# A selective-scan kernel: a step of the scan in two halves, each with its own decays, and other work cut at half steps

## The chip, the cores and the metric

The kernel runs on one core of a Trainium2 chip. The metric is the device time of one launch in microseconds (us). Inside the core, five engines work side by side, each with its own queue of instructions: TensorE (PE in the profile; its weight loads are PEld), VectorE (DVE), ScalarE (ACT), GpSimd (POOL) and SyncE (SP), which here only issues DMAs. They meet through semaphores.

## The reference, cut to what matters

The input x is 8 images of 384 channels and 32 x 32 pixels, in fp32. Four layers follow one another, each as `x = x + layer(group_norm(x))`:

```python
# layers 0 and 2: a Mamba block over the 1024 pixels of an image, 768 inner channels, 16 states each
xin, z = split(xseq @ in_proj_w.T)
u  = silu(causal_conv3(xin) + conv_b)
dt, Bm, Cm = split(u @ x_proj_w.T);  dt = softplus(dt @ dt_proj_w.T + dt_proj_b)
def step(h, inp):
    dA = jnp.exp(dt_t[..., None] * A)                      # the decay of each state
    h = dA * h + (dt_t * u_t)[..., None] * B_t[:, None, :]
    y = jnp.einsum('bdn,bn->bd', h, C_t)
    return (h, y)
y = (scan(step) + u * D) * silu(z);   out = y @ out_proj_w.T
# layer 2 has a layer norm ahead of this and an MLP (384 -> 1536 -> 384, gelu) behind it
# layer 1: 1x1 conv, filter in the frequencies of 8x8 patches, 3x3 depthwise conv, gated, 1x1 conv
# layer 3: 3x3 depthwise conv
```

## The kernel before

**Chunks and steps.** An image is scanned in two chunks of 512 pixels, c = 0 and c = 1; the second starts from the states that the first leaves in `carry`. With 8 images and two Mamba layers there are 32 chunks, numbered n: 0 to 15 belong to layer 0, 16 to 31 to layer 2. A chunk has 768 x 16 states; 128 partitions hold 8 channels x 16 states, and a step scans four such groups, j = 0 to 3, so a chunk has 24 steps and the kernel 768. Three steps in four continue the same block k of 128 channels (`QUADS`).

**One step**, in the loop at the end (L1007 to L1039), t being the step:
- `times` (L619), GpSimd: `g`, which a DMA (`begin`, L610) has filled with dt*u copied over the states, is multiplied by B, in two instructions.
- `decay` (L627), TensorE and ScalarE: four matmuls, each on its own 32 rows of the array, copy dt over the states into the four PSUM banks `dA0` to `dA3`; then four Exp make the decays in place. There is one set of these banks, so the matmul for j of step t+1 must wait until VectorE has done with `dA[j]` of step t.
- `scan` (L637), VectorE: four scans. Those of j = 0 and 1 (`SHARE`) are written over `dA[j]` and VectorE multiplies them by C (L654); those of j = 2 and 3 are written over `g`, and GpSimd multiplies both by C in one instruction (L660) once the last is there. Where c = 0 the last column goes to `carry` (L653, L656).
- `gather` (L664), TensorE: four matmuls sum over the states into `y`; after the fourth step of a block one more adds u*D, and VectorE multiplies y by the gate (L676).

**All else** (norms, projections, gates, output projection, layer 1, MLP, layer 3) is written as generators in a list, `Jobs` (L90). A generator yields after a piece of work. `mm` and the `Meter` count what a piece takes of TensorE and VectorE, in us of a full-speed engine. In each step `jobs.begin` sets the room, `ROOM` (5.2 us of TensorE and 3.0 of VectorE in layer 0, 6.4 and 3.0 in layer 2), and pieces are taken in the order of the jobs' ends (`last`, in steps) while they fit. `NEXT` keeps a job back until the next step, `EARLY` marks a piece that is run right after the scan (a Silu or Gelu, with table loads), `WAIT` says that it can't go on. `jobs.until` runs pieces in order of their ends, past any room, until something that the scan needs is there.

**What sets the order.** [...] TensorE's part of step t is: jobs (up to 2.0 us), `gather` of t-1, the DMA of t+3 (`begin`, on SP), more jobs, and then the four decays of t+1. VectorE's is: the four scans and two multiplications of t, the vector part of the jobs, the gate. A piece of a job usually holds both a matmul group and the VectorE instruction that reads its result (`both`, L222), so the two are issued next to each other.

**Names used below.** `front` prepares a chunk (load, group norm, `layer_norm`, `ps_in`, Silu, `ps_x`, `ps_dt`), `gates` makes z, `finish` holds the output projection and, in layer 2, the MLP; `measure` takes the statistics of the next image through two buffers `spm`, which `layer_norm` and the `ps_dt` part of `front` use too; `live["spm"]` keeps them apart. `NBANK` (3) PSUM banks, `ps`, serve all jobs.

Of the kernel before, what the change touches and what calls it, by code (L numbers as in the profile page):

```python
# [16 lines left out]
P = 128  # L17
# [9 lines left out]
T = 512  # L27
# [21 lines left out]

SHARE = {"l0_": ((2, 2, 2, 2), (2, 2, 2, 2)), "l2_": ((2, 2, 2, 2), (2, 2, 2, 2))}  # L50
# [13 lines left out]
WAIT = "wait"  # L64
NEXT = "next"
EARLY = "early"

ROOM = {"l0_": (5.2, 3.0), "turn": (6.4, 3.0), "l2_": (6.4, 3.0)}
# [21 lines left out]
class Jobs:  # L90
# [3 lines left out]

    def __init__(self, work):
        self.work, self.jobs, self.needs = work, [], {}
        self.room = [0.0, 0.0]

    def add(self, kind, gen, first, last):
        self.jobs.append({"kind": kind, "gen": gen, "first": first, "last": last, "had": [], "got": None})  # L100
# [5 lines left out]
    def piece(self, job):  # L106

        before = list(self.work)
        got = next(job["gen"], self)
        if got is WAIT:  # L110
            return False
        took = tuple(x - y for x, y in zip(self.work, before))
        job["had"].append(took)
        self.room = [x - y for x, y in zip(self.room, took)]
        job["got"] = got
        if got is self:
            self.needs[job["kind"]] = job["had"]
            self.jobs.remove(job)
        return True
# [4 lines left out]
    def begin(self, room):  # L124
        self.room = [max(min(x, y / 8), -y) + y for x, y in zip(self.room, room)]
        early = [job for job in self.in_order() if job["got"] is EARLY]
        for job in self.jobs:
            if job["got"] is NEXT:
                job["got"] = None
        if early:  # L130
            self.piece(early[0])

    def step(self, t, most=None):

        most = most and self.work[0] + most
        went = True
        while went and not (most and self.work[0] >= most):
            went = False
            for job in self.in_order():
                need = self.need(job)  # L140
                if job["got"] is None and job["first"] <= t and all(
                    y == 0 or x >= y - 0.1 for x, y in zip(self.room, need)
                ):
                    went = self.piece(job)
                    if went:
                        break

    def until(self, done):

        while not done():  # L150
            if not any(self.piece(job) for job in self.in_order()):
# [4 lines left out]
def tile_conv_preact_d4(ctx: ExitStack, tc: tile.TileContext, a: dict, out: bass.AP):  # L156
# [10 lines left out]
    live = {"ps": 0, "dt": 0, "x": 0, "spm": False}  # L167
# [21 lines left out]
    def pipe(units, deep=2):  # L189
# [3 lines left out]
        units = deque(units)  # L193
        while units or flying:
            went = bool(flying)
            for f in list(flying):
                if f["stages"]:
                    f["stages"].popleft()(f["ps"])
                settle(f)
                if not f["stages"]:  # L200
                    flying.remove(f)
            if units and live["ps"] < NBANK and len(flying) < deep:
# [4 lines left out]
                stages[0](ps)  # L207
                f = {"stages": deque(stages[1:]), "ps": ps, "bank": True}
                settle(f)
                if f["stages"]:  # L210
                    flying.append(f)
            if units or flying:
                yield None if went else WAIT

    def settle(f):
        if f["bank"] and (not f["stages"] or f["stages"][0] is None):
            f["bank"] = False
            ps_done()
            if f["stages"]:
                f["stages"].popleft()  # L220
# [59 lines left out]
    def group_stats(block, all_read=lambda: None, between=None):  # L280
# [13 lines left out]
        yield NEXT  # L294
# [69 lines left out]
    def depthwise(pool, rows, todo):  # L364
# [12 lines left out]
        yield NEXT  # L377
        for q, (n, t) in enumerate(taps):
            if t == 0:
                ps = yield from ps_tile("ps_dw")  # L380
            _, window, take = todo[n]
# [5 lines left out]
            if t == 8:  # L387
                take(ps[:rows])
# [10 lines left out]
    def measure(s):  # L399
# [12 lines left out]
        live["spm"] = True  # L412
# [7 lines left out]
        def all_read():  # L420
            live["spm"] = False

        s["stats"] = yield from group_stats(block, all_read, NEXT)
# [36 lines left out]
    def layer_norm(xn):  # L460
        ps = yield from ps_tile("ps_ln")
        for k in range(KC):
            mm(ps, ln_mean, xn[:, k, :], start=k == 0, stop=k == KC - 1)
        for k in range(KC):
            vector.tensor_sub(xn[:, k, :], xn[:, k, :], ps)
        ps_done()
        yield NEXT
        while live["spm"]:
            yield WAIT
        ps = yield from ps_tile("ps_lv")  # L470
        for k in range(KC):
            sq = wk.tile([P, T], F32, tag="spm", name="sq", bufs=2)
            act(sq, xn[:, k, :], AF.Square)
            mm(ps, ln_mean, sq, start=k == 0, stop=k == KC - 1)
        rsqrt(ps, ps, eps_ln)
        yield
# [5 lines left out]
        yield NEXT  # L482
        for k in range(KC):
            act(xn[:, k, :], xn[:, k, :], AF.Identity, bias=ln_b[:, k : k + 1])
        yield NEXT

    def front(s):

        c, n = s["c"], s["n"]
        while n > 0 and ("gates", 1) not in chunks[n - 1]:  # L490
            yield WAIT
# [8 lines left out]
        yield NEXT  # L500
# [18 lines left out]
        def taps(d):  # L519
# [10 lines left out]
            ("ps_in", [both(project(s, d, 0), tap(d), taps(d))]) for d in range(ND)  # L530
        )
        if c > 0:
# [16 lines left out]
        yield NEXT  # L549
        ps = yield from ps_tile("ps_x")  # L550
        for d in range(ND):
            mm(ps[:RX, :], w["x"][:, d, :], u[d], start=d == 0, stop=d == ND - 1)
        dbc = wk.tile([RX, T], F32, tag="dbc", name="dbc")
        act(dbc, ps[:RX, :], AF.Identity, bias=one_row)
        ps_done()
        yield NEXT
# [9 lines left out]
        def step_dt(d):  # L566
# [10 lines left out]
            def plus(ps):  # L577
                v = s["dt"][d] = wk.tile([P, T], F32, tag="dt", name="dt", bufs=NDT)
                vector.scalar_tensor_tensor(v, ps, 0.0, got["m"], ALU.max, ALU.add)

# [11 lines left out]
            return [both(log, plus), None, both(times_u, spill)]  # L592
# [3 lines left out]
        flying = []  # L596
        for d in range(ND):
            while live["dt"] >= NDT or live["spm"]:
                yield WAIT
            live["dt"] += 1  # L600

            flying.append(pipe([("ps_dt", step_dt(d))]))
            flying = [f for f in flying if next(f, f) is not f]
            yield NEXT
        while flying:
            flying = [f for f in flying if next(f, f) is not f]
            yield NEXT
# [19 lines left out]
    def decay(s, i):  # L627
        k, sub = QUADS[i]
        for j in range(4):
            rows = slice(32 * j, 32 * (j + 1))  # L630
            mm(dAs[j], selr[rows, sub, :], s["dt"][k][rows, :])
        if sub == NSUB - 1:
            live["dt"] -= 1
        for j in range(4):
            act(dAs[j], dAs[j], AF.Exp, scale=s["w"]["A"][:, 4 * i + j : 4 * i + j + 1])

    def scan(s, i):  # L637

        g = s["g", i]
        own = SHARE[s["pre"]][s["c"]][i % NSUB]  # L640
        for j in range(4):
            q = 4 * i + j
            nc.vector.tensor_tensor_scan(  # L643
                dAs[j] if j < own else g[:, j, :],
# [6 lines left out]
            if j < own:  # L651
# [3 lines left out]
        if s["c"] < NCH - 1:  # L655
            nc.vector.tensor_copy(  # L656
                carry[:, 4 * i + own : 4 * i + 4].unsqueeze(2), g[:, own:4, T - 1 : T]
            )
        g = g[:, own:4, :]
        nc.gpsimd.tensor_mul(  # L660
            g, g, s["bc"][:, 1, :].unsqueeze(1).to_broadcast([P, 4 - own, T])
        )

    def gather(s, i):  # L664
# [8 lines left out]
        if sub == NSUB - 1:  # L673
            u = s["u"][k // NH][:, k % NH, :]
            mm(y, s["w"]["D"][:, k, :], u, start=False)
            nc.vector.tensor_mul(u, y, s["z", k // NH][:, k % NH, :])  # L676
# [4 lines left out]
    def out_proj(s):  # L681
# [24 lines left out]
        def stages(m):  # L706
            if last:
# [3 lines left out]
                both(part(m, 1), lambda ps: vector.tensor_add(x[:, m, :], ps, x[:, m, :])),  # L711
            ]

        yield from pipe(("ps_out", stages(m)) for m in range(KC))
        s["free"] = True

    def finish(s):

        yield from out_proj(s)
# [6 lines left out]
        if s["pre"] == "l2_":  # L726
            if s["c"] == NCH - 1:
                jobs.add("layer3", layer3(s), 0, t + 3 * NQ - 1)
        elif s["c"] == NCH - 1:
            until = 2 * NQ + 3 if s["n"] == B * NCH - 1 else 3 * NQ - 2  # L730
# [34 lines left out]
    def patch_pair(xl, hb, pp):  # L765
# [28 lines left out]
        return pixels, both(frequencies, filtered), back  # L794

    def layer1(s):
# [3 lines left out]
        for hb in range(H // PS):  # L800
# [11 lines left out]
            yield NEXT  # L812
            for stages in zip(*(patch_pair(xl, hb, pp) for pp in range(2))):
                yield from pipe(("ps_t", [stage]) for stage in stages)
                yield NEXT
        for hf in range(2):
            gate = p1.tile([Q96, 2, 512], F32, tag="acc", name="gate")

            def some(j):
# [9 lines left out]
                return w1dw[:, j, :], window, take  # L829
# [6 lines left out]
            yield NEXT  # L836

            def outward(m):
# [8 lines left out]
                return [both(run, lambda ps: vector.tensor_add(xc, ps, xc))]  # L847

            yield from pipe(("ps_o1", outward(m)) for m in range(KC))
            yield  # L850
# [40 lines left out]
    def mlp(s):  # L891
# [12 lines left out]
        for half in range(2):  # L904
# [30 lines left out]
            yield NEXT  # L935

            def down(m):
# [20 lines left out]
                return [sum_up(0, 0), sum_up(0, 1), sum_up(1, 0), both(sum_up(1, 1), add)]  # L958

            yield from pipe([("ps_dn", down(m)) for m in range(KC)], deep=1)  # L960

    def layer3(s):
# [3 lines left out]
        for k in range(KC):  # L966
# [4 lines left out]
            for hf in range(2):  # L971
# [10 lines left out]
                yield from depthwise(p2, P, [(dw3[:, k, :], window, take)])  # L982
# [23 lines left out]
    decay(*steps[0])  # L1006
    for t in range(total):  # L1007
# [3 lines left out]
        if i == 0:  # L1011
            jobs.add("gates", gates(s, 1), t + 1, t + 8)
            if s["c"] == 0 and n + NCH < len(chunks):
                jobs.add("measure", measure(chunks[n + NCH]), t, t + NQ + 4)
            if later:
                jobs.add("front%d" % (later["pre"] == "l2_"), front(later), t + 3, t + 14)
                jobs.add("gates", gates(later, 0), t + 13, t + NQ + 2)
        if i == 3 and n == B * NCH:
            load_diagonal(s["w"], s["pre"])
        if i % (NH * NSUB) == NSUB:  # L1020
            jobs.until(lambda: ("gates", i // (NH * NSUB)) in s)
        if t + 1 < total:
            times(*steps[t + 1])
        scan(s, i)
        jobs.begin(ROOM["turn" if n == B * NCH else s["pre"]])
        jobs.step(t, 2.0)
        if t > 0:
            p, q = steps[t - 1]
            gather(p, q)
            if q == NQ - 1:  # L1030
                end = 10 if p["pre"] == "l0_" else 23 if p["c"] == 0 else 16
                jobs.add("end%d" % (p["pre"] == "l2_"), finish(p), t + 1, t + end)
        if t + AHEAD < total:
            p, q = steps[t + AHEAD]
            jobs.until(lambda: p.get("dud", {}).get(QUADS[q][0]))
            begin(p, q)
        jobs.step(t)
        if t + 1 < total:
            decay(*steps[t + 1])  # L1039
    gather(*steps[-1])  # L1040
    jobs.add("end1", finish(steps[-1][0]), 0, total)
# [131 lines left out]
```

## Time and profile before

| | |
|---|---|
| median of 3 runs | 7926.02 us (7921.78 to 7940.09) |
| the profiled execution | 7942.61 us, its span 7940.8 us |
| before the first scan / after the last scan | 92.4 us / 192.5 us |
| 14 chunks of layer 0 (n = 2 to 15, 336 steps) | 490.0 to 3574.4 us: 9.18 us a step |
| turn from layer 0 to 2 (n = 16 to 21) | 3574.4 to 5230.4 us |
| 9 chunks of layer 2 (n = 22 to 30, 216 steps) | 5230.4 to 7523.7 us: 10.62 us a step |
| busy in the span: PE, DVE, ACT, POOL | 7334.3, 5717.7, 4052.0, 5639.5 us |

The stretches are read off the timeline: a chunk begins with the first of its 96 scans. A busy engine is one that has an instruction in flight[...].

### The profile page before, as it was taken

The page shows a single profiled execution, that of the slowest core. Times are in us where ns is not written, and L with a number is a line of the kernel's source. Part 1 is how long each engine was busy: PE and PEld are TensorE (multiplying, and loading weights), DVE is VectorE, ACT ScalarE, POOL GpSimd, SP SyncE. Part 2 cuts the span into 40 slices and gives each one's busy share as a digit, 9 for nine tenths or more (in the row PEclk, how much of TensorE's full clock was granted, in tenths as well). Part 3 has the DMA queues.
Part 4 walks back from the last instruction along what each step waited for, and adds up shares of the span by engine and source line. Part 5 has one row for each costly group of instructions (what it writes and reads, how often), then busy time and mean ns, then how long its engine had stood idle before and what let it go on. Part 6 is the DMA issues. An engine that isn't in the chain of part 4 may idle for free. (4 is left out here: it accounts for less than half of the span.)

```text
span 7940.8 us, 76871 instructions
## 1 busy us (share of the span) xinstructions
PE 7334.3 (92%) x25954; PEld 3037.2 (38%) x25954; DVE 5717.7 (72%) x7254; ACT 4052.0 (51%) x6980; POOL 5639.5 (71%) x2710
## 2 busy tenths in 40 slices
PE   7989999999998999989999989999899989999898
PEld 2223333333333333333334444444444444344445
DVE  5988788878787878778737647767767676676770
ACT  4445545555555555554544545555555555555553
POOL 5888888877787878777737746767767667676770
PEclk8888888989898999989889989999999999999999
DMA  5665655555564656556526645666656666565662
GB/s 138 148 148 137 144 135 136 134 133 137 133 149 118 146 129 143 122 141 151 122 69 173 159 121 144 154 158 165 157 134 163 166 149 159 138 171 140 168 157 65
DMA packets 289704, 1122.90 MB, mean 141 GB/s; under 512 B 37402, under 2 KB 91754, under 8 KB 191004
## 3 DMA queue, kind: packets, MB, share of 16 engines
q1 hardware_dynamic: 289308, 1117.98, 57.2%
q8 instruction: 205, 3.36, 0.2%
q14 instruction: 191, 1.56, 0.1%
HBM read 1042.34 MB, written 75.50 MB: 141 GB/s over the span
## 5 line engine op out<-in xcount | busy, mean ns | idle before, releaser
L623 POOL TENSOR_TENSOR g<-g,bc 128x1024 f32<-128x1024 f32 x1536 | 3586.5, 2357 | 181.3 <-DMA g<-dud 164.4
L660 POOL TENSOR_TENSOR g<-g,bc 128x1024 f32<-128x1024 f32 x768 | 1805.8, 2351 | 1609.5 <-DVE carry L656 871.8
L241 ACT ACTIVATE dA<-dA,w_A 128x512 f32<-128x512 f32 x3072 | 1858.3, 661 | 1480.3 <-PE dA L177 1467.3
L177 PE MATMUL dA<-dt,selr 32*128 32x512 f32 x6144 | 1521.9, 676 | 67.8 <-DVE g L654 59.2
L643 DVE TENSOR_TENSOR_SCAN dA<-dA,carry,g 128x512 f32<-128x512 f32 x768 | 986.7, 1285 | 750.5 <-issue 375.4
L643 DVE TENSOR_TENSOR_SCAN dA<-dA,g 128x512 f32<-128x512 f32 x768 | 940.8, 1225 | 554.3 <-ACT dA L241 221.6
L654 DVE TENSOR_TENSOR g<-dA,bc 128x512 f32<-128x512 f32 x1536 | 1054.5, 687 | 29.8 <-DVE dA L643 0.5
L177 PE MATMUL y<-g,sely 128*32 128x512 f32 x6144 | 934.2, 640 | 47.6 <-POOL g L660 42.4
L643 DVE TENSOR_TENSOR_SCAN g<-dA,carry,g 128x512 f32<-128x512 f32 x768 | 940.4, 1266 | 0.0
L643 DVE TENSOR_TENSOR_SCAN g<-dA,g 128x512 f32<-128x512 f32 x768 | 893.7, 1206 | 0.0
L177 PEld LDWEIGHTS dA<-dt,selr 32*128 32x128 f32 x6144 | 452.1, 192 | 947.2 <-DVE g L643 473.9
L177 PE MATMUL ps_up<-t,mw 128*128 128x256 f32 x2304 | 605.4, 411 | 144.4 <-ACT h L241 100.5
L177 PE MATMUL ps_dn<-h,mw 128*128 128x256 f32 x2304 | 566.1, 397 | 67.7 <-DMA mw<-in_l_mlp_w 55.9
L177 PE MATMUL ps_z<-xf,w_in 128*128 128x512 f32 x1152 | 590.0, 653 | 27.8 <-DVE dt L85 24.0
L177 PE MATMUL ps_dw<-tp,diag 96*96 96x512 f32 x1152 | 580.7, 645 | 14.3 <-ACT diag L241 14.3
L177 PEld LDWEIGHTS ps_up<-t,mw 128*128 128x128 f32 x2304 | 444.9, 201 | 371.0 <-ACT h L241 186.7
L177 PE MATMUL ps_in<-xf,w_in 128*128 128x512 f32 x1152 | 556.2, 623 | 25.3 <-DVE u L85 22.0
L177 PE MATMUL ps_out<-u,w_out 128*128 128x512 f32 x1152 | 548.7, 623 | 9.1 <-DVE x L85 9.1
L177 PEld LDWEIGHTS ps_dn<-h,mw 128*128 128x128 f32 x2304 | 436.7, 196 | 260.3 <-issue 121.0
L177 PE MATMUL ps_dw<-xp,diag 128*128 128x512 f32 x864 | 405.4, 620 | 41.0 <-ACT diag L241 40.9
L241 ACT ACTIVATE h<-ps_up,vec 128x256 f32<-128x256 f32 x384 | 177.3, 474 | 442.7 <-PE ps_up L177 442.4
L241 ACT ACTIVATE u<-ps_in,w_vec 128x512 f32<-128x512 f32 x192 | 149.4, 778 | 478.1 <-PE ps_in L177 478.1
(98 smaller groups left out, 6514.5 us busy)
## 6 DMA issues: line engine op xcount, KB each, us to landing
g<-dud SPq DMA_DIRECT2D x768, 1024.0 KB, 7.1
mw<-in_l_mlp_w SPq DMA_DIRECT2D x384, 384.0 KB, 7.2
dud<-du SPq DMA_DIRECT2D x768, 64.0 KB, 1.7
xk<-in_x SPq DMA_DIRECT2D x48, 256.0 KB, 4.1
xf<-in_x SPq DMA_DIRECT2D x16, 768.0 KB, 8.5
x<-in_x SPq DMA_DIRECT2D x16, 768.0 KB, 8.4
x_mid<-x SPq DMA_DIRECT2D x16, 768.0 KB, 4.7
xk<-x_mid SPq DMA_DIRECT2D x48, 256.0 KB, 5.4
```

Source lines behind the costliest of these rows:

```text
L177: nc.tensor.matmul(out_, lhsT, rhs, start=start, stop=stop)
L241: nc.scalar.activation(out_, in_, func, **kw)
L623: nc.gpsimd.tensor_mul(g, g, s["bc"][:, 0, :].unsqueeze(1).to_broadcast([P, 2, T]))
L643: nc.vector.tensor_tensor_scan(dAs[j] if j < own else g[:, j, :], dAs[j], g[:, j, :], 0.0 if s["c"] == 0 else carry[:, q : q + 1], ALU.mul ...
L654: nc.vector.tensor_mul(g[:, j, :], dAs[j], s["bc"][:, 1, :])
L660: nc.gpsimd.tensor_mul(g, g, s["bc"][:, 1, :].unsqueeze(1).to_broadcast([P, 4 - own, T]))
```

## The change

**The step.** `decay` and `scan` take a tuple of j. A step is now: `times` of t+1; scans 0 and 1 of t; decays 0 and 1 of t+1; `gather` of t-1; `begin` of t+3; half a step of jobs; scans 2 and 3 of t; decays 2 and 3 of t+1; the gate of t-1 (`gated`, taken out of `gather`); the other half of the jobs. Scans with odd j are written over `dA[j]` and multiplied by VectorE, those with even j go to `g`; GpSimd's multiplication comes after scan 2, ahead of scan 3. `SHARE` goes.

**The jobs.** `Jobs.begin` and `Jobs.step` become `half`, with a room for each half: 2.2 and 3.2 us of TensorE in layer 0 (5.4 a step), 3.0 and 3.9 in layer 2 (6.9); VectorE 1.0 each. A piece is taken if half of what it needs is there, and what it takes too much is owed. A new mark, `HALF`, keeps a job back until the next half step; it replaces most `NEXT`, and stands between a matmul group and the VectorE instruction that reads it, in `pipe`, `front`, `layer_norm`, `depthwise`, `out_proj`, layer 1 and the MLP. `EARLY` pieces run at the beginning of a second half.

**The list.** `out_proj` becomes a job of its own, with its end 6 steps after the chunk; `finish` (MLP) is added when it is done. Other ends: `gates` 4 steps (before 8), `front` 11 (14), layer 1 and layer 3 8 to 11 steps earlier. `until` takes the job that is waited for first. `live["spm"]` counts, so that two `ps_dt` units are under way at a time, and in `layer_norm` the squares are made ahead of the matmuls that read them.

```diff
-    def begin(self, room):
-        self.room = [max(min(x, y / 8), -y) + y for x, y in zip(self.room, room)]
...
+    def half(self, t, room, early):
+
+        self.now += 1
+        self.room = [min(x, 1.5) + y for x, y in zip(self.room, room)]
+        for job in self.in_order():
+            if early and job["early"] and job["at"] <= self.now:
+                self.piece(job)
+                break
...
+                    and all(y == 0 or x >= y / 2 for x, y in zip(self.room, self.need(job)))
...
-    def until(self, done):
+    def until(self, done, kind=None):
         while not done():
-            if not any(self.piece(job) for job in self.in_order()):
+            late = [job for job in self.in_order() if job["kind"] == kind]
+            if not any(self.piece(job) for job in late + self.in_order()):
...
-    def decay(s, i):
+    def decay(s, i, js):
         k, sub = QUADS[i]
-        for j in range(4):
+        for j in js:
             rows = slice(32 * j, 32 * (j + 1))
             mm(dAs[j], selr[rows, sub, :], s["dt"][k][rows, :])
...
-    def scan(s, i):
+    def scan(s, i, js):
...
-                dAs[j] if j < own else g[:, j, :],
+                dAs[j] if j % 2 else g[:, j, :],
...
+            elif j:
+                if s["c"] < NCH - 1:
+                    nc.vector.tensor_copy(
+                        carry[:, 4 * i : 4 * i + 4 : 2].unsqueeze(2), g[:, 0:4:2, T - 1 : T]
+                    )
+                nc.gpsimd.tensor_mul(
+                    g[:, 0:4:2, :], g[:, 0:4:2, :],
+                    s["bc"][:, 1, :].unsqueeze(1).to_broadcast([P, 2, T]),
+                )
...
-        scan(s, i)
-        jobs.begin(ROOM["turn" if n == B * NCH else s["pre"]])
-        jobs.step(t, 2.0)
-        if t > 0:
-            p, q = steps[t - 1]
-            gather(p, q)
...
-        jobs.step(t)
-        if t + 1 < total:
-            decay(*steps[t + 1])
+        scan(s, i, (0, 1))
+        if t + 1 < total:
+            decay(*steps[t + 1], (0, 1))
+        if t > 0:
+            gather(*steps[t - 1])
+        if t + AHEAD < total:
+            p, q = steps[t + AHEAD]
+            jobs.until(
+                lambda: p.get("dud", {}).get(QUADS[q][0]), "front%d" % (p["pre"] == "l2_")
+            )
+            begin(p, q)
+        jobs.half(t, room[0], False)
+        scan(s, i, (2, 3))
+        if t + 1 < total:
+            decay(*steps[t + 1], (2, 3))
...
+            gated(p, q)
             if q == NQ - 1:
-                end = 10 if p["pre"] == "l0_" else 23 if p["c"] == 0 else 16
-                jobs.add("end%d" % (p["pre"] == "l2_"), finish(p), t + 1, t + end)
...
+                jobs.add("out%d" % (p["pre"] == "l2_"), out_proj(p), t + 1, t + 6)
+        jobs.half(t, room[1], True)
```

## The prediction

> **What bounds the kernel now.** I read first the page's busy times, its slices and the busy times by stretch.
>
> ```profile
> PE 7334.3 (92%) x25954; PEld 3037.2 (38%) x25954; DVE 5717.7 (72%) x7254; ACT 4052.0 (51%) x6980; POOL 5639.5 (71%) x2710
> ...
> PE   7989999999998999989999989999899989999898
> ...
> PEclk8888888989898999989889989999999999999999
> ```
>
> ```profile
> core 0: us, PE busy (x) PEld busy (x) DVE busy (x) ACT busy (x) POOL busy (x), PEclk, DMA share, GB/s
> ...
> 490.00:3574.40 3084.40, 2924.42 (x9739) 1032.04 (x9736) 2483.98 (x3148) 1628.03 (x2930) 2464.30 (x1184) 0.90 0.57 136
> ...
> 5230.40:7523.70 2293.30, 2106.55 (x8197) 990.84 (x8196) 1601.66 (x2081) 1214.05 (x2005) 1584.57 (x759) 0.96 0.61 154
> ```
>
> TensorE is the busiest engine everywhere. A layer-0 step (336 in the first stretch) takes 9.18 us: VectorE is busy 7.39 of it, GpSimd 7.33. A layer-2 step (216) takes 10.62: 7.42 and 7.34. So no other engine sets the pace on average, and in layer 0 TensorE's clock is 0.90. The next view is TensorE's decays alone (same columns, PE first), and three pieces of its timeline.
>
> ```profile
> 490.00:3574.40 3084.40, 762.70 (x2687) 227.24 (x2688) 2075.26 (x2353) 816.96 (x1345) 0.90 0.57 136
> 5230.40:7523.70 2293.30, 313.68 (x1728) 91.47 (x1728) 1333.71 (x1537) 517.90 (x865) 0.96 0.61 154
> ```
>
> ```profile
> 3006.21 2.00 PE L177 MATMUL dA<-dt,selr 32*128 32x512 f32 x8
> ```
>
> ```profile
> 5762.99 1.14 PE L177 MATMUL dA<-dt,selr 32*128 32x512 f32 x8
> 5764.06 2.84 PE L177 MATMUL ps_dw<-xp,diag 128*128 128x512 f32 x6
> ```
>
> Decays keep TensorE busy 762.7/336 = 2.27 us a step in layer 0, 313.7/216 = 1.45 in layer 2. With all four banks free they need 1.07 us until the next matmul starts (5762.99 to 5764.06). The rest, 1.20 us a step in layer 0, is waiting for VectorE that the busy time hides. The waits say the same, and show the other direction:
>
> ```profile
> ACT dA L241 <- PE dA L177: 1467.3, 852, 16.8
> ...
> DVE dA L643 <- issue: 553.5, 258, 11.4
> PEld dA L177 <- DVE g L643: 473.9, 668, 1.7
> ...
> DVE dA L643 <- ACT dA L241: 346.9, 123, 9.1
> ...
> DVE acc L85 <- PE ps_dw L177: 233.8, 35, 20.8
> ```
>
> TensorE waits for the last scan and then VectorE for TensorE and Exp. VectorE also waits for job results ("acc <- ps_dw") with scans queued behind. In the worst place a forced `front` holds all scans for 20 us:
>
> ```profile
> 3303.91 4.41 DVE L85 SCALAR_TENSOR_TENSOR u<-ps_in,w_vec,u 128x511 f32<-128x511 f32 x6
> ...
> 3328.61 0.69 DVE L85 SCALAR_TENSOR_TENSOR dt<-ps_dt,spm 128x512 f32<-128x512 f32 x1 [13.56 <-ACT spm L241]
> ...
> 3331.03 1.23 DVE L643 TENSOR_TENSOR_SCAN dA<-dA,g 128x512 f32<-128x512 f32 x1
> ```
>
> [...]
>
> **The change part by part.** The sum is made on the profiled execution (7942.6 us; 7940.8 of it span); it lies 16.6 us above the median, which is taken off at the end.
>
> *Decays in pairs: a cost.* Two pairs in place of one four, each with two rounds: 2 x 1.07 = 2.14 us. Bounds for the pair: 0.54, half of the four, if time went with the count; 1.07, if rounds set it. I take 1.07[...].
> - Layer 0: TensorE without decays 2924.4 - 762.7 = 2161.7; with 336 x 2.14 = 719 it is 2881, against 3084: room for 203 us.
> - Layer 2: 2106.6 - 313.7 = 1792.9; with 216 x 2.14 = 462 it is 2255, against 2293: room for 38 us only. Here 1.45 us become 2.14, on the bounding engine.
>
> *The turnaround goes off the path: the gain.* Exp of scans 0 and 1 of t+1 runs while VectorE is at scans 2 and 3 of t. A half of VectorE is 1.28 + 1.28 + 0.69 + a carry = about 3.4 us; pair and two Exp take 1.07 + 2 x 0.66 = 2.4, so about 1 us is spare. But TensorE now meets VectorE twice a step. Half A holds for it 1.07 + gather 1.00 + jobs 2.2 (3.0) = 4.3 (5.1) us, half B 1.07 + 3.2 (3.9) = 4.3 (5.0); both are over 3.4, and balanced. Pieces are lumps of up to 2.6 us (three matmuls, six records of 0.43), so some meetings miss. The mean wait at a meeting, w, isn't in this trace: 0, if the lumps are absorbed by the 1 us spare; 0.6, half of today's 1.20, if each meeting inherits its share. I take 0.12, near the lower end, because the forced pieces and the waits for job results go too (below). That is 0.24 x 336 = 81 us in layer 0 and 52 in layer 2.
>
> *Vector work a half step later.* Removed are stalls of the kind "acc <- ps_dw" (233.8), "dt <- spm" (143.9), "x <- ps_dn" (140.8); no instruction is added. A `ps` bank is held half a step longer; with three of them the price, if TensorE runs out of banks, is one late piece. Both go into w.
>
> *Gather, begin, gate, multiplication by C.* Gather moves ahead of the first jobs and behind two decays; what it reads was made a half step earlier. `begin` with its 1 MB DMA (7.1 us) goes out earlier on SP, nearly a step more than it needs. GpSimd starts L660 one scan and a multiplication (2.0 us) earlier, its 7.3 us a step then stand against 8.5; the price if it is late is its 164 us of waiting for `g`, today small. Gate and the L656 copy only change place. x and the MLP's weights are still loaded where `out_proj` starts, which in layer 2 is earlier in the chunk; their 8.4 and 7.2 us lie beside its 15 us of matmuls. All at 0.
>
> *Ends, until, squares ahead.* `until` took 33.4 us at the place shown, of which TensorE idled some 10, and VectorE's debt then made light steps; gone, but that is in the room counted above. `ps_lv` took 76.7 + 40.2 idle = 117 us for 16 uses, 7.3 each, against 6 x 0.43 = 2.6; I credit 3 us a use, 27 in the nine layer-2 chunks. The turn takes 1656 us for six chunks, 126 more than six of layer 2 (3 x 510); an earlier layer 1 takes perhaps half of that: 60.
>
> *Clock.* [...] Bounds: no change, or 0.95 and 0.98. I take 0.93 in layer 0 (2161.7 x 0.03/0.93 = 70) and 0.97 in layer 2 (19).
>
> *Sum.* Layer 0: 203 - 81 + 70 = 192 for 14 chunks, 219 for 16. Layer 2: 38 - 52 + 27 + 19 = 32 for nine, 36 for ten. Turn 60. Together 315: 7942.6 - 315 - 16.6 = 7611, said as 7610. Prologue and tail (92.4 and 192.5) stay.
>
> **The rivals.**
> - *Much faster.* w near 0 and clocks 0.95 and 0.98: layer 0 203 + 114 = 317, 362 for 16; layer 2 38 + 27 + 37 = 102, 113 for ten; turn 60: 7390. For it: VectorE and GpSimd leave 1.8 us a step free. Against: their sum per step is steady, the lumps of TensorE are not.
> - *Slower: two meetings a step.* Without the clock's help the gain is 203 x 16/14 + 65 x 10/9 + 60 = 364 us, and each us of w costs 672 x 16/14 + 432 x 10/9 = 1248. So it decides at w = 0.29 us. For it: TensorE can't run ahead past a decay, so a late VectorE job or a 5.5 us Silu piece on ScalarE (two table loads of 1.28, two Silu of 1.48) holds it twice; layer 2 has hardly any room. At w = 0.45 with the turn unchanged: 364 - 60 - 562 = -258, 8180. Against: the balance of the halves.
> - *No difference*: layer 0's gain paid back in layer 2, w near 0.29: 7926.
> - *The pair is cheaper than 1.07* (a decay doesn't do what I say): at 0.54 the 768 steps need 1.07 less each, and with TensorE the bound about half of that shows: 7200; it stands at the far end of much faster.
>
> **How the numbers follow.** Forecast 0.50 (its own range 7430 to 7800), much faster 0.18, no difference 0.07, slower 0.25. Below 7330 I leave about 0.07, above 8120 about 0.12. What a measurement can tell from no change is about 0.2%, 16 us. Faster by more: 0.50 + 0.18 + 0.02 of no difference = 0.70; same 0.03; slower 0.25 + 0.02 = 0.27.
>
> **What would show it.** TensorE's decays near 2.14 us a step in both layers, with a pair at 1.07 to the next matmul; layer-0 steps near 8.6 us, layer-2 steps near 10.5; the clock in layer 0 over 0.90; VectorE's waits for decays and job results less than half; no 20 us gap between scans. It is wrong if the decays' busy time grows past 2.5 us a step (w is large), if the decays' waits only change their name, or if forced pieces come at other steps.

## The result and the profile after

The changed kernel takes 8395.12 us, median of four runs (8390.97 to 8396.11); the kernel before took 7933.06 us beside it (7921.78 to 7941.47). The ratio is 1.0582, with a 95% interval of 1.0564 to 1.0601: slower by 462 us, where 7610 had been forecast. The profiled execution took 8390.97 us, its span is 8389.2.

First the page of the kernel after: busy times, two rows of the slices, and the shares of the chain that ended last.

```profile
PE 7936.0 (95%) x25954; PEld 3189.9 (38%) x25954; DVE 5783.4 (69%) x7254; ACT 4099.6 (49%) x6980; POOL 5631.2 (67%) x2710
...
PE   7999999999999999999999999999999999999998
...
PEclk7778989898989989888899999998999999999999
...
PE 78%; DVE 10%; ACT 7%; issue 2%; POOL 1%; DMA 1%; SPq 0%; POOLq 0%; DVEq 0%; ACTq 0%
```

As many matmuls as before keep TensorE busy 602 us longer (7936.0 against 7334.3). Its idle time fell from 606 to 453 us. 602 less 153 is the 449 us that the span grew. TensorE is still the engine that sets the end, and its clock did not rise: 0.903 over the span, 0.919 before.

Next the stretches, all engines first (layer-0 chunks 2 to 14, 312 steps; layer-2 chunks 22 to 29, 192 steps), then the decay banks alone, where the first number after the length is TensorE's.

```profile
core 0: us, PE busy (x) PEld busy (x) DVE busy (x) ACT busy (x) POOL busy (x), PEclk, DMA share, GB/s
550.50:3640.20 3089.70, 2954.90 (x9238) 1022.72 (x9230) 2360.61 (x2970) 1558.44 (x2793) 2288.78 (x1107) 0.90 0.52 126
5543.30:7700.40 2157.10, 2074.44 (x7316) 947.99 (x7312) 1442.78 (x1824) 1082.29 (x1769) 1405.27 (x676) 0.93 0.58 146
```

```profile
550.50:3640.20 3089.70, 921.88 (x2496) 246.00 (x2496) 1948.62 (x2209) 780.24 (x1248) 0.90 0.52 126
5543.30:7700.40 2157.10, 523.30 (x1536) 144.55 (x1536) 1202.08 (x1344) 476.12 (x769) 0.93 0.58 146
```

A layer-0 step takes 3089.7/312 = 9.90 us, a layer-2 step 2157.1/192 = 11.23. The decays keep TensorE busy 2.95 and 2.73 us a step. What they need when all is ready is seen in the timeline of TensorE in layer 2:

```profile
5555.53 1.13 PE L184 MATMUL dA<-dt,selr 32*128 32x512 f32 x4
5556.59 4.15 PE L184 MATMUL ps_dn<-h,mw 128*128 128x256 f32 x18
```

From the start of the pair (two matmuls, four records) to the next matmul it is 1.06 us: two ready pairs need 2.12 us, and 2.95 less 2.12 is in the main waiting inside the decays. The next table splits a step so for both kernels and for what the prediction had said. "Wait" is TensorE's: decays' busy time less 1.07 us (four at once) or 2.14 us (two pairs, at the predicted price), plus idle time. "Rest" is all its other busy time. Chunks are 2 to 14 and 22 to 30; the predicted rows are worked from the prediction's sums.

| us a step | decays ready | wait | rest | step |
|---|---|---|---|---|
| layer 0 before | 1.07 | 1.64 | 6.46 | 9.16 |
| layer 0 predicted | 2.14 | 0.24 | 6.23 | 8.61 |
| layer 0 after | 2.14 | 1.25 | 6.52 | 9.90 |
| layer 2 before | 1.07 | 1.25 | 8.30 | 10.62 |
| layer 2 predicted | 2.14 | 0.24 | 8.09 | 10.47 |
| layer 2 after | 2.14 | 1.04 | 8.04 | 11.22 |

So the decays' price came out as predicted, and the wait did not go: it fell by 0.39 and 0.21 us a step, where the second pair costs 1.07. The prices are those at a granted clock of 1.00. In stretches at half speed (a granted clock of 0.50) a ready pair took 2.0 us (the median of 60 pairs of the kernel after), and 9% of its decay records in these chunks stand in such stretches; by this estimate some 0.17 us a step of its wait is slow pairs and not waiting. Where the wait sits is seen in VectorE's waits, two lines of the kernel before and then the kernel after (us in total, times, longest):

```profile
DVE dt L85 <- ACT spm L241: 143.9, 37, 16.4
...
DVE u L676 <- PE y L177: 48.7, 37, 4.7
```

```profile
DVE g L686 <- ACT dA L260: 453.7, 232, 11.3
DVE dt L88 <- ACT spm L260: 406.6, 150, 13.6
DVE u L724 <- PE y L184: 304.2, 132, 12.1
DVE x L88 <- PE ps_dn L184: 269.4, 73, 44.6
DVE acc L88 <- PE ps_dw L184: 181.5, 35, 20.8
DVE u L88 <- ACT u L260: 147.4, 40, 7.7
```

All waits of scans, summed over all lines of this view, fell from 1303 to 627 us. All others rose from 839 to 1899: `dt` from 144 to 407, the gate (`u <- y`, L676 before and L724 after) from 49 to 304. The half-step delay was to do away with these.

Two pieces of the timeline of the kernel after show one such stop, VectorE's first, then TensorE's:

```profile
2955.78 0.68 DVE L697 TENSOR_TENSOR g<-dA,bc 128x512 f32<-128x512 f32 x1
2963.20 0.69 DVE L88 BATCH_NORM_STATS2 st<-xk 128x6 f32<-128x512 f32 x1 [6.74 <-DMA xk<-in_x]
2963.81 1.21 DVE L686 TENSOR_TENSOR_SCAN g<-dA,g 128x512 f32<-128x512 f32 x1
```

```profile
2957.56 1.07 PE L184 MATMUL y<-g,sely 128*32 128x512 f32 x8
2958.56 5.42 PE L184 MATMUL ps_out<-u,w_out 128*128 128x512 f32 x12
2965.07 1.12 PE L184 MATMUL dA<-dt,selr 32*128 32x512 f32 x2 [1.09 <-DVE g L686]
2967.19 5.71 PE L184 MATMUL dA<-dt,selr 32*128 32x512 f32 x6 [1.00 <-DVE g L697]
2972.83 1.94 PE L184 MATMUL y<-g,sely 128*32 128x512 f32 x8
```

VectorE stands 6.74 us in front of a statistic, with a ready scan behind it in its queue, which starts only after it, at 2963.81. TensorE uses up its half step of jobs (5.42 us) and then waits twice: at 2965.07 for the scan that frees one bank, and at 2967.19 for the multiplication by C that frees another. The block of six records that starts there lasts 5.71 us, and all of it counts as busy. It is one and a half pairs, and here the stop has a second price: the granted clock is 1.00 up to 2966.2 us and 0.50 from there to 2976.4. At 2.0 us for a pair at half speed the block needs about 3.0, an estimate; the rest of it is waiting. The eight `y` records behind it take 1.94 us, where those ahead of the stop took 1.07.

### The profile page after: what moved, and what is told of

It reads as the page before. It is cut to its first block, busy times and chain, and to the rows that moved or that the text cites. A ratio compares the mean times of both kernels' runs of the same rounds, so it can differ in the third digit from the quotient of the medians.

```text
span 8389.2 us, 76990 instructions
## 1 busy us (share of the span) xinstructions
PE 7936.0 (95%) x25954; PEld 3189.9 (38%) x25954; DVE 5783.4 (69%) x7254; ACT 4099.6 (49%) x6980; POOL 5631.2 (67%) x2710
## 4 chain that ended last, share of the span: by engine, by line
PE 78%; DVE 10%; ACT 7%; issue 2%; POOL 1%; DMA 1%; SPq 0%; POOLq 0%; DVEq 0%; ACTq 0%
PE dA L184 19%; PE y L184 11%; PE ps_dw L184 10%; PE ps_dn L184 6%; PE ps_up L184 6%; PE ps_z L184 6%; PE ps_out L184 6%; PE ps_in L184 5%; DVE g L686 3%; PE ps_t L184 3%; DVE dA L686 3%; PE ps_x L184 2%; DVE g L697 2%; ACT spm L260 1%; PE ps_gn L184 1%
## 5 line engine op out<-in xcount | busy, mean ns | idle before, releaser
L260 ACT ACTIVATE dA<-dA,w_A 128x512 f32<-128x512 f32 x3072 | 1915.3, 658 | 2270.9 <-PE dA L184 2192.2
L184 PE MATMUL dA<-dt,selr 32*128 32x512 f32 x6144 | 2248.1, 701 | 270.7 <-DVE g L686 152.3
L686 DVE TENSOR_TENSOR_SCAN g<-dA,carry,g 128x512 f32<-128x512 f32 x768 | 980.3, 1276 | 430.8 <-ACT dA L260 365.1
L184 PEld LDWEIGHTS dA<-dt,selr 32*128 32x128 f32 x6144 | 611.1, 198 | 1531.7 <-DVE g L697 512.1
L686 DVE TENSOR_TENSOR_SCAN g<-dA,g 128x512 f32<-128x512 f32 x768 | 930.8, 1212 | 197.3 <-ACT dA L260 88.7
L184 PE MATMUL ps_up<-t,mw 128*128 128x256 f32 x2304 | 558.0, 390 | 57.1 <-ACT h L260 56.2
L184 PE MATMUL ps_in<-xf,w_in 128*128 128x512 f32 x1152 | 582.8, 649 | 9.9 <-DVE u L88 8.2
L184 PE MATMUL ps_z<-xf,w_in 128*128 128x512 f32 x1152 | 565.3, 633 | 2.7 <-DVE dt L88 2.7
L88 DVE SCALAR_TENSOR_TENSOR u<-ps_in,w_vec,u 128x511 f32<-128x511 f32 (+1 forms) x384 | 286.1, 747 | 268.2 <-ACT u L260 147.4
L88 DVE SCALAR_TENSOR_TENSOR dt<-ps_dt,spm 128x512 f32<-128x512 f32 x192 | 132.3, 689 | 407.0 <-ACT spm L260 406.6
```

What stands on the lines that cost most here:

```text
L88: return call(out_, *args, **kw)
L184: nc.tensor.matmul(out_, lhsT, rhs, start=start, stop=stop)
L260: nc.scalar.activation(out_, in_, func, **kw)
L686: nc.vector.tensor_tensor_scan(dAs[j] if j % 2 else g[:, j, :], dAs[j], g[:, j, :], 0.0 if s["c"] == 0 else carry[:, q : q + 1], ALU.mult, ...
```

## The experiments

The kernel before took 7942 to 7947 us beside these runs. "List" stands for all that the change does to `Jobs`, rooms, ends and pieces, "step" for the order of the loop.

**1. The new list and the new order of the step, with all four decays after the last scan.**

```diff
-        if t + 1 < total:
-            decay(*steps[t + 1], (0, 1))
...
-            decay(*steps[t + 1], (2, 3))
+            decay(*steps[t + 1], (0, 1, 2, 3))
```

> The changed kernel with one part undone: all four decays of the next step stand in one place, after scans 2 and 3; the list of jobs, its half steps and ends stay as changed. The pair's price (a second pair costs TensorE 1.06 us a step, 768 x 1.06 = 814 us) says that it falls from 8395 to about 7700. The second meeting (TensorE can't run ahead past a decay) says about 7950, because the four still wait once. The list (VectorE's work a half step behind) says that it stays over 8200.

8079.36 us, ratio 1.018 (1.0158 to 1.0203). The pairs are 316 of the 462 us, and the rest of the change costs 137 by itself (the kernel before took 9 us more beside this run). Here VectorE waits 1302 us in front of scans and 905 in front of all else. So the 1899 of the kernel after are not the list's: half of them come with the pairs. The gate, in its new place here too, waits 53 us; it is 304 once a pair of decays stands ahead of `gather` in TensorE's queue:

```profile
DVE u L724 <- PE y L184: 53.1, 43, 7.9
```

**2. The same with the four decay matmuls issued twice**, one meeting a step with nearly the work of two pairs.

```diff
         for j in js:
             rows = slice(32 * j, 32 * (j + 1))
             mm(dAs[j], selr[rows, sub, :], s["dt"][k][rows, :])
+        for j in js:
+            rows = slice(32 * j, 32 * (j + 1))
+            mm(dAs[j], selr[rows, sub, :], s["dt"][k][rows, :])
```

> As the first, and the four decays are issued twice in the same place, the second over the first: TensorE pays about 1.0 us a step more and meets VectorE once. The pair's price says within 150 us of the changed kernel's 8395. The second meeting says less than 200 us over the first run.

8818.12 us, ratio 1.1109 (1.1086 to 1.1132), 739 more than run 1.

```profile
5554.27 2.00 PE L184 MATMUL dA<-dt,selr 32*128 32x512 f32 x16
5556.20 5.42 PE L184 MATMUL ps_z<-xf,w_in 128*128 128x512 f32 x12
```

The eight (16 records) take 1.93 us to the next matmul when ready, 0.86 more than four: 660 us in 768 steps. So all of it shows, and some more. Against this run the kernel after is 423 us faster, with 0.19 us a step more work for TensorE (2.12 against 1.93). This is the turnaround's gain: it is real. The waits of VectorE are 2157 us for scans and 848 for all else, which shows where the job waits come from: not from longer decays, but from the second meeting.

The three steps from the kernel before to the one after are then: list +137, work of the decays +739, meeting VectorE twice in place of once -423.

**3. The kernel before with its four decay matmuls issued twice**, the same edit in its `decay`.

> The kernel before with its four decays issued twice in the same place: only TensorE's work grows, by about 1.0 us a step, 770 us in all. The pair's price says 8350 to 8600 (layer 2 pays it whole, layer 0 the larger part). The second meeting says that the waits in the decays (1.2 us a step in layer 0) hide most of it: under 8150.

8454.36 us, ratio 1.0647 (1.062 to 1.0675): 512 us of the 660 show. Waits that the old order had anyway absorb little of it: with 1.93 us for the eight, the wait is 1.73 us a step in layer 0 (1.64 before) and 1.06 in layer 2 (1.25 before). The rest of TensorE's busy time falls, from 6.46 to 6.27 and from 8.30 to 8.14, at a granted clock of 0.91 (0.90) and 0.97 (0.96). So most of what doesn't show lies in this other work.

**4. The old list with the new step in halves.**

```diff
-        scan(s, i)
+        scan(s, i, (0, 1))
+        if t + 1 < total:
+            decay(*steps[t + 1], (0, 1))
         jobs.begin(ROOM["turn" if n == B * NCH else s["pre"]])
         jobs.step(t, 2.0)
...
             begin(p, q)
+        scan(s, i, (2, 3))
+        if t + 1 < total:
+            decay(*steps[t + 1], (2, 3))
...
         jobs.step(t)
-        if t + 1 < total:
-            decay(*steps[t + 1])
```

> The kernel before with the step alone changed: scans and decays in halves, even j to g, the gate after scans 2 and 3; list, rooms, ends and NEXT stay as before. The pair's price and the second meeting both say 8350 to 8500, as the changed kernel. The list says 7800 to 7950.

11275.13 us, ratio 1.4207 (1.4177 to 1.4236). VectorE's waits in it:

```profile
DVE dt L85 <- ACT spm L241: 1312.9, 192, 18.7
DVE u L85 <- ACT xt L241: 689.0, 96, 19.6
```

`dt` waits 192 times, once for every unit there is, 6.8 us each. The old list issues a matmul group and the instruction that reads its result next to each other. With the decays in pairs, that of a piece among the first 2.0 us of jobs stands between the two halves of the scan: VectorE can't go on to scans 2 and 3, for which TensorE waits, before the result is there. Each such piece becomes a meeting of its own. The mean clock in layer 0 falls to 0.76.

**5. The reverse: the new list with a step like the old one** (four scans; half the jobs; `gather`, `begin`, gate; the other half; four decays).

```diff
-        scan(s, i, (0, 1))
-        if t + 1 < total:
-            decay(*steps[t + 1], (0, 1))
+        scan(s, i, (0, 1, 2, 3))
+        jobs.half(t, room[0], True)
...
-        jobs.half(t, room[0], False)
-        scan(s, i, (2, 3))
-        if t + 1 < total:
-            decay(*steps[t + 1], (2, 3))
...
-        jobs.half(t, room[1], True)
+        jobs.half(t, room[1], False)
+        if t + 1 < total:
+            decay(*steps[t + 1], (0, 1, 2, 3))
```

> The new list with the step of the kernel before: four scans, half the jobs, gather, gate, the other half, four decays at the end. If the first run lost its 137 us because VectorE's jobs stand between its scans, this one gives them back and more, as VectorE's parts now follow groups that TensorE has passed: 7750 to 7900. If the list itself (ends, rooms, half needs) is slower, it stays at 8000 to 8100.

8941.16 us, ratio 1.1252 (1.1216 to 1.1287): a miss. VectorE's waits show what is late now:

```profile
DVE g L686 <- issue: 1244.7, 273, 12.2
DVE g L686 <- ACT dA L260: 968.1, 200, 12.7
```

Scans wait 2648 us in all, and TensorE idles 1.45 and 2.02 us a step. A delayed vector part stands behind four scans here, and TensorE's next group of that job (`ps_in` waits 202 us for VectorE, `ps_dt` 136) stands ahead of the decays. That this chain makes the whole loss is a reading, not shown. The new list and the halves of the step need each other: the list with the old step costs 996 us, the halves with the old list 3333, both together 462.

**6. VectorE's part of a job two half steps behind TensorE's**, in `pipe`.

```diff
-                f["at"] = jobs.now + 1
+                f["at"] = jobs.now + 2
```

> The changed kernel with VectorE's parts in the pipelines a whole step behind TensorE's instead of half a step. If VectorE's waits for job results hold TensorE at the decays, it falls by 150 us or more, to under 8250. If TensorE's own work (the second pair) sets the time, it stays within 80 us of 8395; if the three banks run out, it rises.

8296.63 us, ratio 1.0439 (1.0404 to 1.0474): 98 us better than the kernel after. `dt` now waits 106 us in place of 407, but the scans wait 883 in place of 627. So late results are part of the wait; what this delay wins back is about a fifth of the loss.

**7. The statistics of `measure` kept back a whole step**, the stop shown in the timeline.

```diff
-        s["stats"] = yield from group_stats(block, all_read, HALF)
+        s["stats"] = yield from group_stats(block, all_read, NEXT)
```

> The changed kernel with the statistics of the next image one block a step (as before) and not one a half step. If VectorE's waits for these loads (117 us of idle time, up to 6.7 us at once) hold TensorE, it falls by 40 to 100 us; if TensorE's work sets the time, it stays within 20 us of 8395.

8429.67 us, ratio 1.0611 (1.0582 to 1.0641). The waits of the statistics fall from 117 to 31 us and the time doesn't follow; others grow (`dt` from 407 to 432, the gate from 304 to 315). The stop at 2955 us shows the mechanism, but stops in front of statistics are not what makes the sum.

**8. The kernel after with decay matmuls of 256 columns.** The other half of each decay bank keeps what was there, so half of the decays are not computed anew.

```diff
-            mm(dAs[j], selr[rows, sub, :], s["dt"][k][rows, :])
+            mm(dAs[j][:, : T // 2], selr[rows, sub, :], s["dt"][k][rows, : T // 2])
```

> The changed kernel with decay matmuls of 256 columns instead of 512; columns 256 to 511 of the decays are left as they were, so that part of the scan isn't computed. VectorE, ScalarE and the two meetings stay; a pair should cost TensorE about 0.62 instead of 1.06 us, 0.88 us a step or 675 us in all. If the second pair's price is what the change pays, the time falls by 500 to 675 us, to 7720 to 7900. If the meetings set it, it falls by less than 200.

7928.77 us, ratio 0.9978 (0.9969 to 0.9987). A ready pair takes 0.631 us to the next matmul, so two take 1.26, near the 1.07 of the four before. With decays at about the old price the whole change is then worth 0.2%. A ready pair, and then TensorE's decays in layers 0 and 2 (312 and 216 steps):

```profile
5543.81 0.70 PE L184 MATMUL dA<-dt,selr 32*128 32x256 f32 x4
5544.44 5.42 PE L184 MATMUL ps_out<-u,w_out 128*128 128x512 f32 x12
```

```profile
522.50:3459.00 2936.50, 605.78 (x2496) 259.07 (x2496) 1947.17 (x2209) 781.14 (x1248) 0.89 0.55 133
5247.40:7514.50 2267.10, 379.66 (x1730) 164.85 (x1732) 1349.19 (x1536) 537.56 (x865) 0.94 0.62 157
```

They are busy 1.94 and 1.76 us a step, 0.68 and 0.50 over what two ready pairs need, with idle times of 0.80 and 0.61 beside it. Of the 656 us that were taken off TensorE (0.854 x 768), 466 came out of the time. In layer 0 the wait grew from 1.25 to 1.48 us: part of what the shorter decays save there turns into waiting.

**9. Runs 1 and 6 together**, four decays at once and the vector part two half steps behind.

> The first run (four decays in one place, new list) with VectorE's parts in the pipelines a whole step behind. The whole step took 98 us off the changed kernel; if it works on VectorE's waits for results, it takes 50 to 120 off here too (8079 to about 7990). If it only helps where TensorE meets VectorE twice, 8079 stays.

8093.79 us, ratio 1.0186 (1.0168 to 1.0203), as run 1. The longer delay helps only where there are two meetings.

**10. The kernel before with the new `until`**, which takes the awaited kind first.

```diff
-            if not any(self.piece(job) for job in self.in_order()):
+            late = [job for job in self.in_order() if job["kind"] == kind]
+            if not any(self.piece(job) for job in late + self.in_order()):
```

> The kernel before with one part of the change: jobs.until takes the front job that is waited for first, and not the job with the nearest end. If the forced 28 to 35 us steps cost only what TensorE idles in them, it gains 20 to 80 us (7860 to 7920); if they are work that has to be done anyway, it stays within 20 us of 7935.

7950.67 us, ratio 1.0003 (0.9991 to 1.0016). No difference.

**11. Run 10 with the layer norm's squares made a step ahead** (half a step in the change); `measure` waits until both `spm` buffers are free, as in the change.

```diff
-        for k in range(KC):
-            sq = wk.tile([P, T], F32, tag="spm", name="sq", bufs=2)
-            act(sq, xn[:, k, :], AF.Square)
-            mm(ps, ln_mean, sq, start=k == 0, stop=k == KC - 1)
+        sqs = [square(k) for k in range(2)]
+        yield NEXT
+        ps = yield from ps_tile("ps_lv")
```

> As the run before, and the squares of the layer norm are made a step ahead of their matmuls, with measure kept out of the two buffers meanwhile. My sum credits 3 us a chunk of layer 2, 16 x 3 = 48 us; if the wait is hidden anyway, nothing is gained.

8102.45 us, ratio 1.0198 (1.0173 to 1.0223). A layer-2 step goes from 10.62 to 11.30 us. The place itself gains: `ps_lv` takes 51.5 us and 9.0 of idle time, where it took 76.7 and 40.2. In the old list this part alone is a loss all the same; a likely reason, not shown by itself, is that `layer_norm` holds both `spm` buffers longer and `front` comes later.

**12. The kernel after with its projections and filters cut into pieces of one matmul**, to see whether TensorE's lumps make the wait (one of five places shown; `ps_z`, `ps_x`, `ps_out` and the filter taps likewise; `ps_in`, `ps_z` and `ps_out` also take their units in turn, `in_turn`).

```diff
-            ("ps_in", [both(project(s, d, 0), tap(d)), HALF, taps(d)]) for d in range(ND)
+            ("ps_in", [*project(s, d, 0)[:2], both(project(s, d, 0)[2], tap(d)), HALF, taps(d)])
```

> The changed kernel with its pieces of three matmuls (2.6 us) cut into pieces of one (0.85 us): ps_in, ps_z, ps_x, ps_out and the depthwise taps. If lumps of TensorE's work make the waits at the two meetings (0.56 us each in layer 0), they fall to about half and the time by 200 to 400 us, to 8000 to 8200. If the waits are VectorE's and ScalarE's (results, Silu with table loads), it stays within 80 us of 8395.

8631.6 us, ratio 1.0869 (1.0837 to 1.0901), slower than the kernel after by 236 us. The decays' busy time stays at 2.92 and 2.72 us a step, and TensorE's idle time in layer 2 rises from 0.45 to 0.75. Smaller lumps, cut in this way, don't take the waiting out of the decays.

**13. The kernel before with the new ends of layer 1 and layer 3 only.**

```diff
-                jobs.add("layer3", layer3(s), 0, t + 3 * NQ - 1)
+                jobs.add("layer3", layer3(s), 0, t + 2 * NQ + 14)
...
-            until = 2 * NQ + 3 if s["n"] == B * NCH - 1 else 3 * NQ - 2
+            until = 2 * NQ - 8 if s["n"] == B * NCH - 1 else 2 * NQ + 14
```

> The kernel before with nothing but earlier ends for layer 1 and layer 3 (62 steps in place of 70 and 71, 40 in place of 51 for the last layer 1). The changed kernel's tail is 20 us shorter (172.4 against 192.6) and its turn 0.56 us a step shorter even without the pair's price. If that comes from the ends, this gains 20 to 90 us (7860 to 7925); if it comes from the half steps or from out_proj as its own job, it stays within 15 us of 7945.

8033.87 us, ratio 1.0111 (1.0087 to 1.0136). The turn gets shorter (11.20 to 10.87 us a step), but layer 0 and layer 2 get longer (9.36 and 10.81), and what is left after the last scan grows from 192.6 to 241.5 us. A likely reading, not shown, is that earlier ends push the same work to places that have no more room. In the full change the tail is shorter, 172.4 us.

## Why the prediction was wrong

**Decays in pairs: right.** Priced at 1.07 us, measured at 1.06; the bound of 0.54 (time going with the count) is out. The reason is in the timelines: decays issued together, each on 32 rows of its own, overlap. Three matmuls on all 128 rows took 2.84 us from start to end (`ps_dw` at 5764.06 in the kernel before), four decays just ahead of them 1.14, and the two at 5555.53 in the kernel after 1.13. So two pairs cost nearly what two fours would (2.12 us against 2.14). One decay alone is no cheaper: it took 1.12 us at 2965.07, and a lone `y<-u,w_D` on all rows at 5548.51 also 1.12. Run 2 (739 us more than run 1) and run 8 (466 less than the kernel after) show that the time follows the decays' length, whichever way it is changed.

**The turnaround: the step that failed.** It is w, the mean wait at a meeting: "I take 0.12, near the lower end, because the forced pieces and the waits for job results go too." Measured is 1.25/2 = 0.62 us a meeting in layer 0 and 1.04/2 = 0.52 in layer 2. TensorE's idle time is in these, as the prediction's sum needs it: it had counted all idle time as room. Inside the decays alone, where its upper bound of 0.6 (half of 1.20) belongs, it is 0.41 and 0.30. So w lies near that bound in the one count and at half to two thirds of it in the other, and in both well over 0.12. The sign that the prediction had set for a large w, decays over 2.5 us a step, came: 2.95 and 2.73. The gain is there (423 us, run 2 against the kernel after), but it is less than the second pair costs.

With 0.62 and 0.52 the slower rival's own sum gives 364 - 60 - 768 x 0.62 - 480 x 0.52 = -422, that is 8348, 47 under the measured time. Some of this nearness is luck: in it a layer-0 step is 0.16 us too short and a layer-2 step 0.13 too long. But the named rival was the right one, and w lies well past the 0.29 from which it decides.

**Why the wait stayed.** The prediction took it that VectorE's waits for job results are stalls that the half-step delay removes. They doubled, from 839 to 1899 us. Runs 1 and 2 have the same list and one meeting, and show 905 and 848. So it is the second meeting that makes results late: TensorE's jobs now stand behind a pair of decays in each half, that pair waits for VectorE, and VectorE a half step later waits for the jobs. The gate, costed at nothing, is the plainest piece of it: 49 us before, 53 in run 1, 304 after.

The traces, read back from TensorE's stops, agree. In chunks 2 to 14 of the kernel after, TensorE stood at the decays 98 times for over 1 us more than ready ones need, 0.95 us a step together. In 94 of these (0.90 us) the last idle time of VectorE over 0.3 us ahead of the stop's end was one in front of a job's result; in the kernel before, in 24 of 91 (0.27 of 0.98). In layer 2 it is 28 of 40 stops, before none of 39. No single result leads: the largest in layer 0, `dt`, stands ahead of 27 stops, 0.24 us a step, and the gate ahead of 8, 0.08. This also fits run 7, where one kind went and the sum stayed.

What is not settled is how much of a stop is the late result and how much VectorE's own work: in layer 0 it was busy in 1.04 of the 1.06 us a step that TensorE stood for over 0.3 us, working off what had gathered. A rival is therefore open: that VectorE's work per half, with scans, statistics and jobs, comes in lumps. Run 6 gives 98 us to late results. Moving the gate alone, smaller lumps of VectorE's work, or a second set of decay banks, was not tried.

**Idle time.** The sums for both layers took it that TensorE's idle time goes (0.45 and 0.86 us a step were in the "room"). Left are 0.43 in layer 0 and 0.45 in layer 2.

**The clock.** 0.93 and 0.97 were estimates of the author's; it is 0.90 and 0.93, so the 70 and 19 us did not come, and layer 2 lost instead. Here half speed goes with long stops more than with the whole wait. In layer 2 the wait fell from 1.25 to 1.04 us a step and the clock fell too, from 0.96 to 0.93, but stops of over 2 us at the decays rose from 0.24 to 0.58 us a step (19 stops before, 33 after). In layer 0, where the clock stayed at 0.90, they are 0.87 before and 0.76 after.

**Until, squares, ends.** `until` at nothing was right (run 10). The squares were credited with 3 us a use, and at their place gave 4: all uses of `ps_lv` took 117 us with the idle time ahead of them, and take 51 in the kernel after.

```profile
L177 PE MATMUL ps_lv<-sq,ln_mean 128*128 128x512 f32 x96 | 76.7, 962 | 40.2 <-ACT sq L241 40.2
```

```profile
L184 PE MATMUL ps_lv<-sq,ln_mean 128*128 128x512 f32 x96 | 50.1, 646 | 0.7 <-ACT sq L260 0.4
```

Whether the kernel's time gained by it is open: alone in the old list this part cost 150 us (run 11). The rest of layer 2's busy time did fall, by 0.26 us a step, but no run says by which part; in run 1, which has the squares too, it is 8.34. The turn (n = 16 to 21) was to give 60 us and gave 16, 1640 us in place of 1656; with chunk 15, which grew from 225 to 263 us, it takes 11.33 us a step in place of 11.20. Run 13 shows a shorter turn from the ends alone, but paid for elsewhere.

**Balance.** Against the profiled execution, the sum (7610 + 16.6 = 7626.6) misses 764 us. Layer 0 is 384 x 1.29 = 495 of it, layer 2 240 x 0.75 = 180, the turn 44 (1640 us against 1596); some 45 are left: chunks 0, 1, 15 and 31 lost more than these means, and the tail, 20 us shorter, gives part of it back. In layer 0 the 1.29 us are 1.00 of wait, and 0.29 of a rest that was to be shortened by the clock.

## What to carry to other kernels

Splitting a dependent pair of engines into two meetings a step pays only if the time saved at the turnaround is more than what the split instructions cost on the bounding engine: here 423 us against 739. Let today's wait stand at nearly its whole sum until a run shows less (here 1.25 of 1.64 us a step stayed in layer 0, and 1.04 of 1.25 in layer 2), and don't count a wait as removed because its instruction is issued later: ask what the producer now stands behind. When an engine is 92% busy, first find out how much of that is waiting inside its instructions: by the prediction's estimate 1.20 us a step in layer 0 here, more than its idle time.

## What the runs showed of the hardware

- The time of a pair of decays does not halve with its columns: a ready one takes 1.058 us to the next matmul with 512 columns (the kernel after) and 0.631 with 256 (run 8). A straight line through the two, an estimate, puts 0.427 on each 256 columns and leaves about 0.2. Eight decay matmuls in one go take 1.93 us (run 2), less than two pairs (2.12).
- Half speed also follows records that look busy. The kernel before has 187 stretches at a granted clock of 0.50, 1287 us in all. Over the 5 us ahead of each, about half a step, TensorE was busy 68% of the time on average, against 92% over windows of this length laid end to end. But 34% of the stretches followed a window with 90% or more, and in these the decays' records were 61% of the time, against 20% in all such busy windows. The kernel after has 181 stretches, 1621 us; there it is rarer and weaker, 18% of the stretches and 39% against 26%.
- A ready pair takes 2.0 us at a granted clock of 0.50 (the median of 60) and 1.06 at 1.00, both in the kernel after.
